# Two graph layers on one core: wk and wv loaded behind the first turn of x, q computed before k, and all places written anew

## The chip, the cores and the metric

The kernel runs on one core of one Trainium2 chip. The metric is the device time of one execution in microseconds (us), as the median of several runs. The core has a matmul engine (PE, with its weight loads PEld), a vector engine (DVE), a scalar engine (ACT), GpSimd (POOL) and SyncE (SP), which here only issues transfers (DMAs).

## The reference, cut to what is computed

```python
# x: (128, 128, 512) float32, adj: (128, 128) of zeros and ones
q, k, v = (x @ Wq + bq), (x @ Wk + bk), (x @ Wv + bv)        # 8 heads of 64
scores = einsum('bqhd,bkhd->bhqk', q, k) / sqrt(64) + (1 - adj) * -1e9
x = layernorm(x + einsum('bhqk,bkhd->bqhd', softmax(scores), v) @ Wo + bo)

h = x @ W                                                    # (512, 512)
s1, s2 = h @ a[:512], h @ a[512:]
e = leaky_relu(s1[:, :, None] + s2[:, None, :], 0.2) * adj
h_prime = softmax(e, axis=2) @ h
x = layernorm(x + elu(h_prime + beta * h))
```

The output has the shape of x. All is float32.

## The kernel before

The 128 batches (b) are worked on in 64 pairs (g, with b0 and b1). For a pair and each of the five weights (q, k, v, w for Wo, h for W) the product of the 512-wide x of two batches with the weight is a 2 x 2 block product made of seven block products instead of eight: `product(name, g, n)` with n from 1 to 7 (L293 for v, w and h, L299 for q and k). Products 1 and 2 need only plain blocks of the weight and of x; the others need sums of blocks. `weight_sum(name, n, engine)` (L215 to L221) makes the sums of a weight once, on DVE for q and k and on POOL for v, w and h; `block_sum` (L252, POOL) makes those of x (tx), oT and zT for each pair. The results leave PSUM by `take_part` (ACT for q, k, v and h at L347 and L341, DVE for w at L344), with a first copy into qT, kT, v, y or h, and by `add_block` (L357, DVE), which adds a second block to it. The PSUM pool has 8 buffers, so a product also waits until an earlier result has been taken out. Seven block products of q or k are 8 matmul passes each.

A pair goes through these stages: x is fetched twice, once in blocks of 32 rows (`load_blocks` L81, tile xblk, one buffer, four transfers) which `turn_x` (L232, DVE, one call for each batch) transposes into xT, and once as rows (`load_x` L91); then the q and k products, `scores` (L371), `mask` (L379) and `row_max` (L387) on DVE, `exps` (L393) and `normalise` (L407) on ACT; the attention weights go to memory and come back (`attn_write` L414 and `attn_read` L419, issued by SP), and are turned by DVE (`turn_attn` L436); `attend` (L446) follows, the w products, a layernorm, the second layer's row sums (`row_product` L497, `s2_write` L540, `s2_read` L548), its weights (`weights_write`, `weights_read`), `aggregate` (L634), the h products, elu (`elu_max` L649 on DVE, `elu_exp` L645 on ACT), a layernorm (`norm_f` L664) and `store` (L670, SP). The stages of several pairs overlap.

The order on every engine is written by hand. `at(place, fn, args)` puts a step on a list with a place, a number; the list is sorted by place and executed in that order with the scheduler switched off, so each engine and each queue executes its instructions in order of place. A pair's steps are in `rows(g)`, in which the places count from `g * STEP` (36.678). Pairs 62 and 63 have `last_rows`, where w and h of the last pair are computed as plain products. The dictionary `other` gives pairs 0, 1, 2, 3, 60 and 61 other places for the same rows. Steps that happen once (weight sums, loads of later weights) have places of their own.

At the start, outside this list, SP issues the first x in blocks and then wq, wk and wv (each 1 MB, `load_turned` L99); ACT issues two more quarters of x; POOL issues the small inputs (adj, the biases, a). `keep_busy(20, "early")` (L137) gives PE matmuls on an identity matrix, 40 passes in the profile, until data come. The function `load_later` fetches the rows of the first batches. wo and w1 follow by `load_weight` (L121). `wa_column` (L179, DVE), `wa_turn` and `wa_centre` make the product of W with the vectors a, once.

Of the kernel before, what the change touches and what calls it, by code (L numbers as in the profile page):

```python
# [18 lines left out]
STEP = 36.678  # L19
# [3 lines left out]
def gnn_two_layers(  # L23
# [91 lines left out]
    load_turned(wk_sb, wk)  # L115
    load_turned(wv_sb, wv)
# [22 lines left out]
    keep_busy(20, "early")  # L139
# [65 lines left out]
    sums = {}  # L205

# [475 lines left out]
    def at(place, fn, *args):  # L682
        pieces.append((place, len(pieces), fn, args))

    def rows(g):

        b0, b1 = g * G, g * G + 1
        return (
            (-44.716, fetch_blocks, g), (-36.858, turn_x, g, 0), (-32.016, turn_x, g, 1),
            (-29.266, block_sum, "x", g, 1), (-28.714, block_sum, "x", g, 2),  # L690
            (-26.46, block_sum, "x", g, 4), (-25.056, block_sum, "x", g, 3),
            (-21.919, product, "q", g, 1), (-21.658, take_part, "q", g, 1, 0, 0),
            (-19.5, product, "k", g, 1), (-17.956, product, "q", g, 2),
            (-16.658, take_part, "k", g, 1, 0, 0), (-15.381, product, "q", g, 6),
            (-15.182, add_block, "q", g, 2, 0, 0), (-14.288, product, "k", g, 2),
            (-12.099, take_part, "q", g, 6, 1, 0), (-11.378, product, "k", g, 6),
            (-10.677, product, "q", g, 7), (-10.463, product, "k", g, 7),
            (-9.776, add_block, "k", g, 2, 0, 0), (-9.113, take_part, "k", g, 6, 1, 0),
            (-6.848, product, "q", g, 5), (-6.525, product, "k", g, 5),
            (-6.518, take_part, "q", g, 5, 1, 1), (-6.421, take_part, "k", g, 5, 1, 1),  # L700
            (-5.969, add_block, "q", g, 7, 1, 1), (-5.586, fetch_x, b0), (-5.534, fetch_x, b1),
            (-4.88, product, "q", g, 3), (-4.75, add_block, "k", g, 7, 1, 1),
            (-3.315, product, "k", g, 3), (-2.944, product, "q", g, 4),
            (-2.923, take_part, "k", g, 3, 0, 1), (-2.725, take_part, "q", g, 3, 0, 1),
            (-1.262, product, "k", g, 4), (-0.719, add_block, "k", g, 4, 1, 0),
            (-0.692, add_block, "q", g, 4, 1, 0), (1.869, residual, b1), (2.023, scores, b0),
            (2.943, scores, b1), (3.203, product, "v", g, 1), (3.463, mask, b0, 0),
            (3.487, mask, b0, 1), (3.658, row_max, b0), (4.555, exps, b0, 0),
            (5.075, mask, b1, 0), (6.271, residual, b0), (6.383, product, "v", g, 2),
            (6.541, exps, b0, 1), (7.568, take_part, "v", g, 1, 0, 0), (7.611, exps, b0, 2),  # L710
            (8.122, product, "v", g, 7), (8.183, mask, b1, 1), (8.41, product, "v", g, 6),
            (8.797, exps, b0, 3), (8.894, add_block, "v", g, 2, 0, 0),
            (8.955, take_part, "v", g, 6, 1, 0), (9.854, row_inv, b0),
            (10.401, normalise, b0, 0), (10.555, normalise, b0, 1), (10.857, normalise, b0, 2),
            (11.052, row_max, b1), (11.513, normalise, b0, 3), (11.654, attn_write, b0),
            (11.776, product, "v", g, 5), (12.497, exps, b1, 0), (13.24, exps, b1, 1),
            (15.283, attn_read, b0), (16.447, exps, b1, 2), (17.972, exps, b1, 3),
            (18.187, row_inv, b1), (20.285, normalise, b1, 0), (20.649, normalise, b1, 1),
            (20.984, normalise, b1, 2), (22.744, normalise, b1, 3), (22.805, attn_write, b1),
            (24.259, turn_attn, b0, 0), (25.642, take_part, "v", g, 5, 1, 1),  # L720
            (25.922, attn_read, b1), (28.935, add_block, "v", g, 7, 1, 1),
            (30.213, product, "v", g, 3), (30.509, product, "v", g, 4),
            (31.14, take_part, "v", g, 3, 0, 1), (31.481, turn_attn, b0, 1),
            (31.923, add_block, "v", g, 4, 1, 0), (32.495, turn_attn, b1, 0),
            (32.689, turn_attn, b1, 1), (35.816, attend, b0), (36.86, attend, b1),
            (37.764, attend_evict, b0), (38.489, attend_evict, b1),
            (40.162, block_sum, "w", g, 1), (40.287, block_sum, "w", g, 3),
            (40.532, product, "w", g, 1), (41.714, product, "w", g, 2),
            (43.07, block_sum, "w", g, 2), (43.121, take_part, "w", g, 1, 0, 0),
            (43.685, block_sum, "w", g, 4), (44.107, add_block, "w", g, 2, 0, 0),  # L730
            (46.18, product, "w", g, 6), (47.336, take_part, "w", g, 6, 1, 0),
            (47.833, product, "w", g, 7), (48.561, product, "w", g, 5),
            (49.902, take_part, "w", g, 5, 1, 1), (50.317, add_block, "w", g, 7, 1, 1),
            (51.85, product, "w", g, 3), (52.678, take_part, "w", g, 3, 0, 1),
            (52.954, product, "w", g, 4), (53.025, bn_stats, y, b1, "c"),
            (54.273, add_block, "w", g, 4, 1, 0), (54.685, bn_stats, y, b0, "c"),
            (56.257, bn_aggr, b1, "c"), (57.446, bn_aggr, b0, "c"), (57.581, add_eps, g, "c"),
            (57.665, inv_std, g, "c"), (57.668, row_product, b1, 0),
            (57.799, row_product, b0, 0), (59.124, row_product, b1, 1),
            (59.504, row_product, b0, 1), (59.697, scale_s, g), (59.806, s2_turn, g),  # L740
            (61.509, s2_write, g), (63.81, norm_c, b0), (63.847, s2_read, g),
            (65.062, norm_c, b1), (69.697, edge, g, 0), (70.127, edge, g, 1), (70.179, leaky, g),
            (70.643, edge_max, g), (72.113, edge_exp, g), (73.622, edge_inv, g),
            (74.481, weights, g, 0), (75.191, weights, g, 1), (76.181, weights_write, g),
            (78.597, weights_read, g), (84.328, weights_turn, g), (85.331, aggregate, b0),
            (86.702, aggregate, b1), (87.456, aggregate_evict, b0),
            (88.848, aggregate_evict, b1), (89.224, block_sum, "h", g, 1),
            (90.935, product, "h", g, 1), (92.58, take_part, "h", g, 1, 0, 0),
            (92.618, block_sum, "h", g, 2), (93.008, product, "h", g, 2),
            (95.183, product, "h", g, 6), (95.377, block_sum, "h", g, 3),  # L750
            (95.522, take_part, "h", g, 6, 1, 0), (96.049, product, "h", g, 5),
            (96.355, product, "h", g, 7), (96.647, add_block, "h", g, 2, 0, 0),
            (98.71, block_sum, "h", g, 4), (99.498, take_part, "h", g, 5, 1, 1),
            (100.462, add_block, "h", g, 7, 1, 1), (101.867, product, "h", g, 4),
            (102.513, product, "h", g, 3), (102.514, take_part, "h", g, 3, 0, 1),
            (102.524, add_block, "h", g, 4, 1, 0), (103.384, elu_max, b0), (103.53, elu_exp, b0),
            (104.737, elu_max, b1), (107.392, elu_exp, b1), (118.64, elu_sum, b0),
            (120.181, bn_stats, u, b0, "f"), (121.875, elu_sum, b1), (122.064, bn_aggr, b0, "f"),
            (124.368, bn_stats, u, b1, "f"), (124.757, bn_aggr, b1, "f"),
            (125.543, add_eps, g, "f"), (129.855, inv_std, g, "f"), (131.762, shift, g),  # L760
            (132.875, norm_f, b1), (133, norm_f, b0), (133.412, store, b1), (133.946, store, b0),
        )

    def last_rows(g):

        b0, b1 = g * G, g * G + 1
        if g == NG - 2:
            return (
                (-44.716, fetch_blocks, g), (-36.858, turn_x, g, 0), (-32.016, turn_x, g, 1),
                (-29.266, block_sum, "x", g, 1), (-28.714, block_sum, "x", g, 2),  # L770
                (-26.46, block_sum, "x", g, 4), (-25.056, block_sum, "x", g, 3),
                (-20.581, product, "q", g, 7), (-19.688, product, "q", g, 1), (-18.819, fetch_x, b0),
                (-18.555, take_part, "q", g, 1, 0, 0), (-17.929, product, "k", g, 1),
                (-17.919, fetch_x, b1), (-17.036, product, "k", g, 7), (-16.143, product, "k", g, 2),
# [261 lines left out]

    for g in range(NG):
        lay(g)
    at(-0.85, load_later)
    at(7.15, make_mask)  # L1040
    at(7.47, weight_sum, "k", 3, nc.vector)
    at(8.19, weight_sum, "k", 1, nc.vector)
# [69 lines left out]
```

## Time and profile before

| | us |
|---|---|
| three runs | 2390.34, 2392.12, 2392.55 |
| median | 2392.12 |
| profiled execution, whole time | 2389.93 |
| its span (the profile's time axis) | 2388.1 |
| PE busy | 2359.0 (99%) |
| DVE, ACT, POOL busy | 79%, 66%, 36% |
| period of a middle pair | 36.50 |
| first product of x on PE | 13.12 |
| last matmul ends | 2379.43 |

The time axis of the profile begins with the program. In the lists of PE in order of time a line has the start, the time taken, engine, line of the code, output and inputs, how many instructions it holds, and in brackets the idle time ahead of it and what ended it. In a table of stretches each engine has its busy time and the number of instructions, then follow the granted clock of PE (1.00 is full speed), the busy share of the 16 DMA engines and GB/s. In a list of waits the numbers are us in total, times, longest.

### The profile page before, as it was taken

Reading aid. Unit: us, or ns where it says so; the run is one execution under the profiler, and the core shown is the slowest. Engines: PE = TensorE matmul, PEld = TensorE weight load, DVE = VectorE, ACT = ScalarE, POOL = GpSimd, SP = SyncE. Lnnn points to the kernel's source line nnn. Section 1 sums busy time; section 2 is a strip of 40 time slices with the busy share of each in tenths; the row PEclk is TensorE's granted clock in tenths of the full one; section 3 lists DMA queues with packets and bytes.
Section 4 is the critical chain, followed back from the end, with each engine's and each line's share of the span. In section 5 each row is a group of like instructions: output and inputs, shape, how many; then the busy total and the mean of one; then the engine's idle time right before and its main releaser. Section 6 shows DMA issues by size and latency. Waiting matters only on the chain.

```text
span 2388.1 us, 50634 instructions
## 1 busy us (share of the span) xinstructions
PE 2359.0 (99%) x17708; PEld 2179.7 (91%) x17708; DVE 1876.4 (79%) x4381; ACT 1583.2 (66%) x5760; POOL 867.2 (36%) x1047
## 2 busy tenths in 40 slices
PE   8999999999999999999999999999999999999998
PEld 7898999999999999999999999999999999999985
DVE  6787787877877877878778778778788787787877
ACT  4676766766666666667666676676676666766655
POOL 6242433433433334334334333343343343333421
PEclk9999999999999999999999999999999999999999
DMA  6333334344343343343433433433434334334332
GB/s 191 103 95 115 108 104 132 92 120 124 101 119 114 103 125 105 106 132 93 120 121 103 119 112 105 125 100 111 133 91 120 117 107 118 107 111 125 118 100 73
DMA packets 255905, 269.82 MB, mean 113 GB/s; under 512 B 57425, under 2 KB 204369, under 8 KB 255265
## 3 DMA queue, kind: packets, MB, share of 16 engines
q1 hardware_dynamic: 254704, 265.45, 37.0%
q8 instruction: 140, 2.29, 0.4%
q14 instruction: 117, 0.95, 0.1%
q0 software_dynamic: 400, 0.86, 0.1%
q10 hardware_dynamic: 544, 0.26, 0.0%
HBM read 157.62 MB, written 108.85 MB: 112 GB/s over the span
## 4 chain that ended last, share of the span: by engine, by line
PE 95%; DMA 2%; DVE 1%; ACT 1%; SPq 0%; issue 0%; DVEq 0%; ACTq 0%
PE pv L293 12%; PE pk L299 12%; PE pq L299 11%; PE pw L293 11%; PE ph L293 11%; PE eq L299 9%; PE psc L371 5%; PE po L446 5%; PE pz L634 5%; PE ew L293 4%; PE ev L293 4%; PE eh L293 4%; DMA scr<-sb 1%; ACT sb L407 1%; DMA ab<-scr 1%; DMA wk_sb<-in_L_gnn_Wk_dram 0%
## 5 line engine op out<-in xcount | busy, mean ns | idle before, releaser
L393 ACT ACTIVATE s<-s,nmax 128x128 f32<-128x128 f32 x1024 | 398.1, 395 | 150.1 <-DVE nmax L387 150.1
L427 POOL TENSOR_TENSOR x<-x,bo_b_in 128x512 f32<-128x512 f32 x128 | 163.8, 1280 | 892.6 <-DMA x<-in_x_dram 769.9
L407 ACT ACTIVATE sb<-s,rinv 128x128 f32<-128x128 f32 x1024 | 319.5, 395 | 2.9 <-DMA scr<-sb 2.6
L347 ACT ACTIVATE kT<-pk,bk_c 128x128 f32<-128x128 f32 x512 | 160.6, 367 | 194.1 <-PE pk L299 151.5
L341 ACT COPY h<-ph 128x256 f32<-128x256 f32 x252 | 94.6, 376 | 258.4 <-PE ph L293 257.1
L347 ACT ACTIVATE qT<-pq,bq_c 128x128 f32<-128x128 f32 x512 | 159.2, 364 | 89.7 <-PE pq L299 89.3
L393 ACT ACTIVATION_READ_ACCUMULATOR s<-s,nmax 128x1 f32 x1024 | 196.9, 192 | 0.0
L252 POOL TENSOR_TENSOR th<-zT,zT 128x256 f32<-128x256 f32 x63 | 46.3, 736 | 395.5 <-ACT zT L641 395.5
L379 DVE SCALAR_TENSOR_TENSOR s<-psc,amask 128x512 f32<-128x512 f32 x256 | 167.6, 676 | 27.6 <-PE psc L371 27.3
L344 DVE TENSOR_TENSOR w<-pw,x 128x256 f32<-128x256 f32 x252 | 103.2, 410 | 101.0 <-PE pw L293 100.9
L497 DVE SCALAR_TENSOR_TENSOR ya<-w,wa_row 128x512 f32<-128x512 f32 x256 | 177.6, 694 | 4.4
L436 DVE STREAM_TRANSPOSE attnT<-ab 128x512 f32<-128x512 f32 x256 | 172.6, 694 | 7.4 <-DMA ab<-scr 6.5
L458 ACT ACTIVATE oT<-po,bv_c 128x128 f32<-128x128 f32 x512 | 139.6, 382 | 27.7 <-PE po L446 27.7
L387 DVE TENSOR_REDUCE nmax<-s 128x8 f32<-128x1024 f32 x128 | 153.5, 1199 | 2.3
L232 DVE STREAM_TRANSPOSE xT<-xblk 128x512 f32<-128x512 f32 x128 | 143.1, 1120 | 5.2 <-DMA xblk<-in_x_dram 5.2
L299 PEld LDWEIGHTS pk<-xT,wk_sb 128*128 128x128 f32 x1024 | 136.0, 195 | 10.6 <-issue 4.2
L299 PE MATMUL pk<-xT,wk_sb 128*128 128x128 f32 x1024 | 136.9, 278 | 4.1 <-DMA wk_sb<-in_L_gnn_Wk_dram 4.1
L293 PE MATMUL pv<-wv_sb,xT 128*128 128x256 f32 x512 | 137.6, 391 | 0.0
L299 PE MATMUL pq<-xT,wq_sb 128*128 128x128 f32 x1024 | 134.8, 275 | 0.0
L299 PEld LDWEIGHTS pq<-xT,wq_sb 128*128 128x128 f32 x1024 | 129.4, 192 | 3.3
L371 PE MATMUL psc<-kT,qT 64*128 64x128 f32 x2048 | 131.8, 278 | 0.0
L371 PEld LDWEIGHTS psc<-kT,qT 64*128 64x128 f32 x2048 | 119.4, 188 | 11.5 <-issue 11.3
(674 smaller groups left out, 6297.0 us busy)
## 6 DMA issues: line engine op xcount, KB each, us to landing
scr<-sb SPq DMA_DIRECT2D x128, 512.0 KB
ab<-scr SPq DMA_DIRECT2D x512, 128.0 KB
x<-in_x_dram SPq DMA_DIRECT2D x128, 256.0 KB
out_dram<-u SPq DMA_DIRECT2D x128, 256.0 KB
xblk<-in_x_dram SPq DMA_DIRECT2D x254, 128.0 KB
pb<-s2d SPq DMA_DIRECT2D x62, 128.0 KB
attd<-att SPq DMA_DIRECT2D x62, 128.0 KB
ab<-attd SPq DMA_DIRECT2D x248, 32.0 KB
```

Source lines behind the costliest of these rows:

```text
L232: nc.vector.transpose(xT[g][:, :, t * N : (t + 1) * N].rearrange("p m (b r) -> p b m r", r=Q), xblk[g][:, t].rearrange("p b (c m) -> p b m ...
L293: nc.tensor.matmul(out, b[:, c, :], a[:, c, :], start=first and c == 0, stop=(c == 1), skip_group_check=True,)
L299: nc.tensor.matmul(out[:, m * N : (m + 1) * N], a[:, c, m * P : (m + 1) * P], b[:, c, :], start=first and m == 0 and c == 0, stop=(c == 1) ...
L347: nc.scalar.activation(dst[:, m, :], src[:, m * N : (m + 1) * N], AF.Identity, bias=BIAS[name][:, 2 * i + m : 2 * i + m + 1],)
L371: nc.tensor.matmul(psc[b][j][:, m, :], qT[g][feats, m, rows], kT[g][feats, m, rows], start=True, stop=True,)
L379: nc.vector.scalar_tensor_tensor(s_t[b][:, j * HP : (j + 1) * HP, :], psc[b][j], SCALE, amask.rearrange("p (o n) -> p o n", o=1).broadcast ...
L387: nc.vector.tensor_reduce(nmax[b], s_t[b], AX.X, ALU.max, negate=True)
L393: nc.scalar.activation(s_t[b][:, h, :], s_t[b][:, h, :], AF.Exp, bias=nmax[b][:, h : h + 1], accum_out=rsum[b][:, h : h + 1],)
L407: nc.scalar.mul(sb[b][:, :, h, :], s_t[b][:, h, :].rearrange("p (b c) -> p b c", c=Q), rinv[b][:, h : h + 1],)
L427: nc.gpsimd.tensor_tensor(xr[b], xr[b], later["bo"], ALU.add)
L436: nc.vector.transpose(attnT[b].rearrange("p h (a r) -> p a h r", r=Q)[:, rows], ab[b].rearrange("p a (h c) -> p a h c", c=Q)[:, rows],)
L497: nc.vector.scalar_tensor_tensor(z, y[b], 1.0, wa_row[j], ALU.mult, ALU.mult, accum_out=s12[g][:, i, j : j + 1])
```

## The change

Four things are changed, all in the function that the profile's lines belong to.

1. At the front only wq is loaded. wk and wv are loaded by a new step, which first writes one element of wk's tile in each partition on DVE, so that SP's transfer of wk waits for that instruction. Its place puts it between pair 0's two `turn_x`.
2. `keep_busy(20, "early")` becomes 15.
3. In pair 0 the q products come first: q1, q2, q7, then k1, k2, q6, k7, k6, q5, k5, q3, k3, k4, q4. On DVE the sums of wq come before those of wk. w1 is loaded before wo. The first of pair 1's `turn_x` stands ahead of the additions of q7 and k7 and of products k4 and q4; the first wa_column stands ahead of the additions of k4 and q4. The rows of b0 are fetched directly behind wv.
4. All places are other numbers: those of `rows(g)`, so of every middle pair, of `last_rows`, and of the six pairs in `other`. STEP is the same. The steps are the same, each with the same instructions.

In the middle pairs, for example, the order of the q and k products is q1, k1, q2, q6, k6, k2, q7, k7, q5, k5, q3, k3, q4, k4, where it was q1, k1, q2, q6, k2, k6, q7, k7, q5, k5, q3, k3, q4, k4. Near the end, the attn_read of batch 123 is ahead of an s2_write on SP, and on ACT q5's part is ahead of the elu_exp of batch 118, where each was behind it.

```diff
     load_turned(wq_sb, wq)
-    load_turned(wk_sb, wk)
-    load_turned(wv_sb, wv)
...
-    keep_busy(20, "early")
+    keep_busy(15, "early")
...
+    def load_k_and_v():
+
+
+        nc.vector.memset(wk_sb[:, 0, :1], 0.0)
+        load_turned(wk_sb, wk)
+        load_turned(wv_sb, wv)
...
     def rows(g):
-            (-44.716, fetch_blocks, g), (-36.858, turn_x, g, 0), (-32.016, turn_x, g, 1),
-            (-29.266, block_sum, "x", g, 1), (-28.714, block_sum, "x", g, 2),
...
+            (-44.347, fetch_blocks, g), (-35.5, turn_x, g, 0), (-35.24, turn_x, g, 1),
+            (-33.234, block_sum, "x", g, 1), (-29.664, block_sum, "x", g, 2),
...
     for g in range(NG):
         lay(g)
-    at(-0.85, load_later)
-    at(7.15, make_mask)
-    at(7.47, weight_sum, "k", 3, nc.vector)
...
-    at(10.35, weight_sum, "q", 3, nc.vector)
...
-    at(15.55, load_weight, wo_sb, wo)
...
-    at(18.25, load_weight, w1_sb, w1)
...
-    at(26.53, wa_column, 1, 0)
+    at(0.672, load_later)
+    at(5.774, load_k_and_v)
+    at(8.812, weight_sum, "q", 3, nc.vector)
...
+    at(13.252, weight_sum, "k", 3, nc.vector)
...
+    at(16.882, load_weight, w1_sb, w1)
...
+    at(19.582, load_weight, wo_sb, wo)
...
+    at(22.002, wa_column, 0, 1)
```

## The prediction

> **What bounds the kernel now.** I read the busy shares by slice, then PE's busy time by stretch, then what PE waited for, then PE in order of time.
>
> ```profile
> PE   8999999999999999999999999999999999999998
> ...
> DMA  6333334344343343343433433433434334334332
> ```
> ```profile
> core 0: us, PE busy (x) PEld busy (x) DVE busy (x) ACT busy (x) POOL busy (x), PEclk, DMA share, GB/s
> 0.00:13.12 13.12, 6.36 (x40) 6.19 (x41) 2.42 (x4) 1.28 (x1) 8.76 (x21) 0.99 0.84 271
> 13.12:60.00 46.88, 43.77 (x369) 40.90 (x369) 39.42 (x67) 24.23 (x93) 28.26 (x25) 0.97 0.59 168
> 60.00:240.00 180.00, 175.77 (x1329) 162.62 (x1330) 137.25 (x319) 117.31 (x438) 59.02 (x72) 0.99 0.35 104
> 240.00:2240.00 2000.00, 1999.99 (x15085) 1857.73 (x15084) 1584.51 (x3724) 1353.47 (x4933) 727.80 (x877) 1.00 0.38 113
> 2240.00:2379.43 139.43, 133.15 (x890) 112.30 (x889) 109.36 (x261) 84.78 (x293) 42.34 (x52) 0.99 0.29 95
> 2379.43:2388.10 8.67, 0.00 (x0) 0.00 (x0) 3.42 (x11) 2.16 (x3) 1.08 (x2) 0.64 0.16 60
> ```
>
> TensorE is the bound: in the 2000 us of the middle pairs it lacks 0.01 us, so nothing can be won there, only lost. The rest can be listed: 13.12 before the first product, 3.11 idle to 60, 4.23 to 240, 6.28 to the last matmul, 8.67 behind it.
>
> ```profile
> PE pk L299 <- DMA wk_sb<-in_L_gnn_Wk_dram: 4.1, 1, 4.1
> PE ph L293 <- ACT h L341: 3.4, 4, 2.2
> PE pk L299 <- ACT kT L347: 3.0, 2, 1.9
> ...
> PE pq L299 <- ACT qT L347: 2.5, 1, 2.5
> ```
> ```profile
> 2.70 6.36 PE L137 MATMUL early<-ident 128*128 128x128 f32 x40 [2.70 <-POOL ident masks.py:199]
> 13.12 3.57 PE L299 MATMUL pk<-xT,wk_sb 128*128 128x128 f32 x16 [4.07 <-DMA wk_sb<-in_L_gnn_Wk_dram]
> 17.46 1.13 PE L299 MATMUL pk<-tx,s_k 128*128 128x128 f32 x8 [0.76 <-issue]
> 18.43 1.95 PE L299 MATMUL pq<-xT,wq_sb 128*128 128x128 f32 x16
> ```
>
> The start is a wait for wk: the chain of waits has "DMA wk_sb" from 2.15 to 12.99. wq, issued first, is used only at 18.43. The first 16 passes take 3.57 where 16 warm ones take 1.79 on the chain (clock 0.50 in 13 to 16).
>
> **What the Trainium skill says.** (1) "TensorE: Matmul & The Clock Gate", section "What's actually happening": the clock is halved by default and after an idle window of about 3.4 us, and the window runs freely, so the gap that triggers it varies. The trace agrees and is sharper: gaps of 4.07, 2.47 and 2.16 us were followed by a clock of 0.50, 0.50 and 0.55, gaps of 1.89 and 1.07 by 1.00. (2) "DMA: Bandwidth & Descriptors", "Why a DMA increments its semaphore by 16 and not by 1": a transfer counts as landed only when all its engines are done, and these finish independently. The trace shows this: wk landed at 12.99, though at the mean rates (277 GB/s from 2 to 8, 368 from 8 to 13) the bytes ahead of its end had passed earlier. (3) Same page, "Queues, rings and completion order": an engine takes the descriptors of one queue in ring order. So moving wk's issue on SP back, behind nothing but x and wq, costs only as far as an engine runs dry; no row shows this.
>
> **The change, part by part.** The sum is made against the profiled execution, 2389.93; the median is 2392.12, so 2.2 is added at the end.
>
> *Early passes, 40 to 30.* They ran at 6 to 7 a microsecond to about 6 us and some 11 after, so 30 end near 6.9. Nothing waits for the ten: worth 0 while PE waits for data; their cover is the load of wq.
>
> *q in front of k.* wq is then the first weight. Its landing isn't shown; q1 had moved 1.40 MB by 8.0, against 1.31 for x's half and wq, so I take 8.5 (7.7 to 9.4). Products 1 and 2 of q (1.79) and 7 (0.89) run by 11.3: 2.68 us of work in what was idle. Both remaining gaps are about 1.7, which stayed warm before.
>
> *wk and wv behind a memset.* The memset (one element a partition, estimate 0.1) stands on DVE between the two turns of x, 1.08 us each, the first at 5.24. SP's issue of wk waits for it, so moves from 2.15 to about 6.4, with wv, the second batch of x, four xblk_1 and w1 queued behind it on SP. xblk_1 was issued at 7.35 and goes to about 7.9. At 6.4 the rings still hold half of wq, so I keep wk's landing at 13.0; bounds: 12.3 (two loads no longer interleave with wq) and 17 (the full 4.25).
>
> *From 13.0 on.* Before, 112 passes stood between wk and v1, with 1.78 of cold clock and 0.76 of issue; now 88. Nine products by 0.893 end at 21.0 (k1, k2, q6, k7, k6, q5, k5, q3, k3). Then comes a new wait. The order on DVE is now: turn of pair 1 (waits for xblk_1), add q7, add k7, and k4 needs their place in PSUM. xblk_1 used to be first-quarter landed at 19.90 and was turned at 24.48 without a wait; now it lies behind all of wv, estimate 21.6 (21 to 24). So k4 starts at 21.6 + 1.09 + 2 x 0.42 = 23.5: a gap of 2.5, cold with one chance in two (0.5 x 1.7 = 0.9). k4, q4 1.79, v1 0.86, q1 of pair 1 0.89: scores at 27.0 against 29.39, with one product of 0.89 more behind it: -3.2. wa_column now waits for w1 behind wv on the same DVE; w1 is due near 24.7, add k4 and add q4 stand behind it, and this just fits; not counted.
>
> *To 60.* 44.44 (0.45) and 51.06 (1.89) are stalls of the old order of pair 1, whose ACT order is new; I count the 1.89 as gone. **Start: -3.2 - 1.9 + 0.9 = -4.2**, between -6.5 and 0.
>
> *60 to 240.* Idle 4.23 and 1.7 of cold behind
>
> ```profile
> 217.47 0.48 PE L293 MATMUL ph<-s_h,th 128*128 128x256 f32 x1 [2.16 <-ACT h L341]
> ```
>
> 5.9 in all. The copy of h stood on ACT behind normalise, norm_f and a q/k part. In the new order of pairs 2 to 4 these are spread otherwise, but k6 and q5 follow close on their parts; I keep two thirds as lost: **-2.0**, between -5.9 and +3.
>
> *Middle pairs.* Every place is new, the instructions are the same. The tightest new distance on PE is k3 behind k5's part: 1.76 us of products between them against 0.2 + 0.63 of ACT. Scores, attend and aggregate have over 2 us. DVE is busy 79% and ACT 68% of a period of 36.5. **0**, between 0 and +17 (0.3 a pair); below nothing is excluded by 0.01 us idle.
>
> *End.* The largest stall:
>
> ```profile
> 2278.22 0.63 ACT L645 ACTIVATE h<-h 128x512 f32<-128x512 f32 x1 [3.51 <-DVE u L649]
> ```
> ```profile
> 2276.90 0.71 DVE L436 STREAM_TRANSPOSE attnT<-ab 128x512 f32<-128x512 f32 x1 [3.00 <-DMA ab<-scr]
> ```
>
> DVE waited 3.00 for an attn_read that SP issued at 2272.43 behind two stores (2.03) and an s2_write (1.03); elu_max stood behind it, elu_exp behind that, q5's part behind that on ACT, and PE waited 2.47 and ran cold (1.7). In the new order the read is ahead of the s2_write and q5's part ahead of elu_exp: -4.2. What is late next isn't known: the last five pairs have other new orders, with 3.8 of small stalls now. I take half: **-2.0**, between -5 and +4. The 8.67 behind the last matmul is the same chain of elu_sum, statistics, norm_f and store: 0.
>
> Sum -4.2 - 2.0 + 0 - 2.0 = -8.2: profiled run 2381.7, median 2383.9, say 2384.0.
>
> **The rivals.** *No gain (A):* the start is bound by bytes, not by their order: the DMA share is 0.97 to 1.12 from 2 to 31 us, and wk, wv, xblk_1, w1 and wo are the same bytes. Then xblk_1 lands at its bound of 24, k4 starts at 25.9, runs cold (1.7), and after 3.54 us of k4, q4, v1 and q1 the scores begin at 31.1: 0.9 late against 29.39 + 0.89. With the 1.89 gone the start gives -1.0; pairs 1 to 3 and the end find other stalls of the old size: 2389.93 - 1.0 + 2.2 = 2391.1. For it: the share. Against it: the 2.68 us of q work that no later byte delays.
>
> *Slower (B):* one new wait in the repeated order. A place on ACT or DVE that is late by 0.1 us in each middle pair costs 0.1 x 56 = 5.6 and leaves 2.6 of the gains; from 0.15 a pair (8.4) the kernel is slower, and at 0.25 it is 14.0 - 8.2 = +5.8: 2398. For it: PE has no slack to hide anything (1999.99 of 2000), and attention's round trip of write (2.6 to 4.6) and read (3.7) is measured against a new place of turn_attn. Against it: the old middle order shows no wait at all at the same busy shares, and I find no new distance shorter than its work.
>
> *Full gain (C):* xblk_1 in time, gaps warm, no new stalls outside: -6.5 - 5 - 4 = 2376.6.
>
> *The issue doesn't move (D):* were SP to issue wk early all the same, nothing would be lost, since q still starts first: 2384, the forecast.
>
> **How the numbers follow.** Forecast and C together 0.62 (C 0.12), A 0.25, B 0.13. 0.2%, 4.8 us, is about what a measurement of this kernel can tell from no change: faster is below 2387.3, slower above 2396.9. Forecast and C lie below, A between, B mostly above. The range leaves out half of C and most of B: 2376.5 to 2392.5.
>
> **What would show it.** First pass of q near 8.5, first of k near 13.0, both at clock 1.00; a wait of 2 to 3 us on DVE for xblk_1 and of k4 on DVE near 21 to 23.5; scores near 27; 2000.0 busy of 2000 in the middle; no stall on "ACT qT" near 2279. Wrong, if wk lands past 14, if the middle shows idle PE over 3 us, or if the last 140 us hold more than 6.3 of idle.

## The result, and the profile after

| | before | after |
|---|---|---|
| median, us | 2390.45 (6 runs, 2390.21 to 2392.55) | 2383.07 (6 runs, 2380.52 to 2384.31) |
| profiled execution, us | 2389.93 | 2381.98 |
| its span, us | 2388.1 | 2380.2 |
| last matmul ends | 2379.43 | 2372.0 |

The ratio is 0.9965 (95% interval 0.9953 to 0.9978): 7.4 us faster by the medians, 7.9 by the spans. The forecast was 2384.0, or 8.2 less than the kernel before.

PE's busy time by stretch, of the kernel after; the columns are those of the table shown of before:

```profile
core 0: us, PE busy (x) PEld busy (x) DVE busy (x) ACT busy (x) POOL busy (x), PEclk, DMA share, GB/s
0.00:8.50 8.50, 5.79 (x27) 5.79 (x28) 2.11 (x3) 0.32 (x1) 7.18 (x19) 1.00 0.73 202
8.50:60.00 51.50, 44.59 (x374) 41.29 (x373) 39.63 (x69) 25.42 (x94) 29.68 (x27) 0.97 0.63 188
60.00:240.00 180.00, 178.23 (x1350) 164.90 (x1349) 146.74 (x325) 119.13 (x450) 64.46 (x77) 1.00 0.36 106
240.00:2230.00 1990.00, 1990.00 (x15029) 1849.02 (x15028) 1654.71 (x3712) 1357.31 (x4915) 724.78 (x872) 1.00 0.37 113
2230.00:2372.00 142.00, 136.67 (x926) 115.89 (x924) 112.83 (x267) 88.38 (x301) 43.84 (x52) 1.00 0.34 102
```

The middle has no idle PE at all, as before. The lost time is idle time and the time that passes at half clock take too long, about 1.7 us behind each gap that ended cold. 13.12 and 10.12 are the times of the first product. By stretch it compares so:

| stretch | before | after | difference | forecast |
|---|---|---|---|---|
| to 60 us, early passes counted as lost | 13.12 + 3.11 + 1.8 = 18.0 | 10.12 + 5.79 + 1.7 = 17.6 | -0.4 | -4.2 |
| 60 to 240 | 4.23 + 1.7 = 5.9 | 1.77 | -4.2 | -2.0 |
| middle | 0.01 | 0.00 | 0 | 0 |
| end, to the last matmul | 6.28 + 1.7 = 8.0 | 5.33 | -2.7 | -2.0 |
| behind it | 8.67 | 8.2 | -0.5 | 0 |

The sum, -7.8, is nearly that of the forecast; its parts are not. The stretch to 240 gave twice what was forecast, the end somewhat more than forecast, and the start next to nothing. PE in the order of time, at the start of the kernel after:

```profile
2.71 6.29 PE L135 MATMUL early<-ident 128*128 128x128 f32 x30 [2.71 <-POOL ident masks.py:199]
10.12 2.02 PE L304 MATMUL pq<-xT,wq_sb 128*128 128x128 f32 x16 [1.12 <-DMA wq_sb<-in_L_gnn_Wq_dram]
14.39 2.05 PE L304 MATMUL pk<-xT,wk_sb 128*128 128x128 f32 x16 [1.35 <-DMA wk_sb<-in_L_gnn_Wk_dram]
...
24.11 1.13 PE L304 MATMUL eq<-tx,wk_sb 128*128 128x128 f32 x8 [0.71 <-DVE kT L362]
...
27.82 2.06 PE L376 MATMUL psc<-kT,qT 64*128 64x128 f32 x32
...
45.44 1.65 PE L298 MATMUL ev<-wv_sb,tx 128*128 128x256 f32 x4 [3.38 <-DVE v L362]
```

The first product starts 3.0 us sooner, PE stays at full clock after both first gaps, and the scores come at 27.82 instead of 29.39 with one product more done: up to there it goes much as forecast. Then PE waits 3.38 us for the addition of v7 and runs at half clock after it (0.57 from 45.4 to 49). What DVE did until then:

```profile
22.20 1.12 DVE L237 STREAM_TRANSPOSE xT<-xblk 128x512 f32<-128x512 f32 x1 [2.55 <-DMA xblk<-in_x_dram]
...
26.29 0.93 DVE L177 SCALAR_TENSOR_TENSOR wa_t<-w_sb,uf_in 128x512 f32<-128x512 f32 x1 [1.30 <-DMA w_sb<-in_L_gnn_W_dram]
...
38.59 1.66 DVE L177 SCALAR_TENSOR_TENSOR wa_t<-w_sb,uf_in 128x512 f32<-128x512 f32 x1
...
41.81 1.49 DVE L197 TENSOR_SCALAR wa_row<-wa_row,wa_mean 128x512 f32<-128x512 f32 x1
```

It waited 2.55 us for xblk_1 (the first blocks of pair 1), as forecast, and 1.30 us for w1, which landed at 26.19 where 24.7 was due. From there to the addition of v7 it hardly pauses, 18.64 us busy of 19.10, and PE is busy for 15.76:

```profile
26.30:45.40 19.10, 15.76 (x128) 14.38 (x126) 18.64 (x34) 11.54 (x50) 15.34 (x13) 1.00 0.45 118
```

In the same stretch of the kernel before DVE is busy for 15.84 us and PE for 18.65. The chain of waits that ends at the product at 45.44 runs over DVE from 26.3 on, but for 3.20 us of exps, and behind that over the landing of w1 (14.94 to 26.19). So w1 sets when DVE begins, and DVE's queue sets when PE goes on.

### The profile page after: what moved, and what is told of

Same layout as the page of the kernel before. It is cut to its first block, busy times and chain, and to the rows that moved or that the text cites. A ratio compares the mean times of both kernels' runs of the same rounds, so it can differ in the third digit from the quotient of the medians.

```text
span 2380.2 us, 50849 instructions
## 1 busy us (share of the span) xinstructions
PE 2355.3 (99%) x17698; PEld 2176.9 (91%) x17698; DVE 1959.5 (82%) x4382; ACT 1592.1 (67%) x5760; POOL 871.4 (37%) x1047
## 4 chain that ended last, share of the span: by engine, by line
PE 95%; DVE 2%; DMA 1%; ACT 1%; SPq 0%; issue 0%; ACTq 0%; DVEq 0%
PE pv L298 12%; PE pq L304 12%; PE pk L304 11%; PE pw L298 11%; PE ph L298 11%; PE eq L304 9%; PE psc L376 5%; PE po L451 5%; PE pz L639 5%; PE eh L298 5%; PE ew L298 4%; PE ev L298 4%; DMA w_sb<-in_L_gnn_W_dram 0%; ACT s L398 0%; DVE wa_t L177 0%; PE plh L333 0%
## 5 line engine op out<-in xcount | busy, mean ns | idle before, releaser
L412 ACT ACTIVATE sb<-s,rinv 128x128 f32<-128x128 f32 x1024 | 325.7, 392 | 5.5 <-DVE rinv L405 4.4
L502 DVE SCALAR_TENSOR_TENSOR ya<-w,wa_row 128x512 f32<-128x512 f32 x256 | 225.2, 880 | 4.3
L346 ACT COPY v<-pv 128x256 f32<-128x256 f32 x256 | 94.5, 369 | 87.1 <-PE pv L298 60.6
L257 POOL TENSOR_TENSOR tx<-xT 128x256 f32<-128x256 f32 x128 | 95.9, 750 | 132.5 <-PE psc L376 106.4
L654 DVE SCALAR_TENSOR_TENSOR u<-h,x 128x512 f32<-128x512 f32 x126 | 87.1, 692 | 61.5 <-ACT h L346 59.3
L304 PEld LDWEIGHTS pk<-xT,wk_sb 128*128 128x128 f32 x1024 | 129.0, 192 | 4.7 <-DMA wk_sb<-in_L_gnn_Wk_dram 1.5
```

The lines of the kernel that those rows point to most:

```text
L304: nc.tensor.matmul(out[:, m * N : (m + 1) * N], a[:, c, m * P : (m + 1) * P], b[:, c, :], start=first and m == 0 and c == 0, stop=(c == 1) ...
L346: nc.scalar.copy(dst, src)
L412: nc.scalar.mul(sb[b][:, :, h, :], s_t[b][:, h, :].rearrange("p (b c) -> p b c", c=Q), rinv[b][:, h : h + 1],)
L502: nc.vector.scalar_tensor_tensor(z, y[b], 1.0, wa_row[j], ALU.mult, ALU.mult, accum_out=s12[g][:, i, j : j + 1])
```

## The experiments

In two kinds: single places of the change put into the kernel before, and single places of the kernel after undone or moved. Each was timed in turn with the kernel before on the same chip; its median differs from chip to chip (2389.6 to 2391.6), so the ratios are compared. Single executions of one kernel differ by more than some of these edits are worth (the kernel before took 2384.03 to 2392.91 in 46 runs on one chip), so a trace shows one execution, and a gain is read from the medians.

**The loads in front again.**

```diff
     load_turned(wq_sb, wq)
+    load_turned(wk_sb, wk)
+    load_turned(wv_sb, wv)
...
-    at(5.774, load_k_and_v)
```

> The kernel after, with wk and wv issued directly behind wq at the front again; all places and the q-first order stay. Theory (ring order): each DMA engine takes wq's descriptors first anyway, so the first q product stays at 10.1 us within 0.7, wk lands about 13.0 instead of 14.3, and the time is 2381 to 2384. Rival (interleaving): three loads in flight at once delay wq, the first q product starts at 11.5 or later, and the start gives back 1.5 us or more: 2385 to 2387.

Measured: 2381.44, ratio 0.9964 (0.9951 to 0.9976). The time is that of the kernel after.

```profile
11.30 3.47 PE L306 MATMUL pq<-xT,wq_sb 128*128 128x128 f32 x16 [2.70 <-DMA wq_sb<-in_L_gnn_Wq_dram]
```

The first q product started at 11.30, behind a gap of 2.70 that ended cold, where it was 10.12. That the loads delay each other is not shown by this: in a later run with all three in front it started at 10.17, and in three later ones with the deferral at 9.29, 10.18 and 11.01. wk was there without a wait when q was done. The scores came at 29.80, 2.0 later than in the kernel after, and yet the time is the same: where the kernel after waits 3.38 us for DVE and goes cold, this one waits 1.46 and 1.54 us for it and stays at full clock. The part that gave the change its name is worth nothing that these intervals, some 3 us to either side, can tell.

**The old start, the new middle and end; and the new end alone.** Both take the rows of both kernels and choose by pair:

```diff
+    new = lambda g: g >= 4        # first kernel;  g >= NG - 4 in the second
...
+        rows, last_rows, other = (
+            (rows_a, last_rows_a, other_a) if new(g) else (rows_b, last_rows_b, other_b)
+        )
```

> The front and pairs 0 to 3 of the kernel before, all later pairs (middle and end) of the kernel after. By the account of lost PE time in the two traces, stretch by stretch, the start to 240 us is worth 4.6 us of the 7.9 and the end 3.1: so 2387.3 against 2390.5 of before. Rival: the end's gain is tied to the start's order, or the switch of order between pairs 3 and 4 costs a stall: 2390 or more.

> The kernel before, with the new places in pairs 60 to 63 alone. If the middle pairs' new order is worth nothing, as the 1990.00 of 1990 us busy says, this equals the run with the old start and the new middle, 2387.3 within 1. Rival: the new middle order carries part of the gain (the DVE order that reaches the end), then this stays near 2390.

Measured: 2392.28, ratio 1.0012 (1.0004 to 1.0020), and 2393.77, ratio 1.0017 (1.0010 to 1.0023). Both were expected at 2387.3 and are slower than the kernel before. PE in order of time in the first of them, around the pairs where the orders meet:

```profile
174.09 1.13 PE L293 MATMUL pv<-wv_sb,tx 128*128 128x256 f32 x4 [1.38 <-ACT v L341]
...
225.36 1.10 PE L293 MATMUL ph<-s_h,th 128*128 128x256 f32 x4 [1.76 <-ACT h L341]
```

There are eight such waits between 147 and 255 us, 6.2 us in all, seven of them for a step on ACT; in the second, waits of 0.3 to 1.4 us stand from 2194 us on. Two orders that each run without a wait in the middle do not fit one another. Steps of several pairs interleave on ACT and DVE there, which is the likely reason; no run shows it by itself. So these kernels can't price a stretch. One thing can be read from the first: its end has the waits of the kernel after (1.54, 0.55, 0.16, 0.81 and 0.50 us; in the kernel after 1.50, 0.55, 0.46, 0.81 and 0.50, with one of 0.18) although its start is the old one. The end's gain doesn't hang on the start.

**wk issued ahead of wq, in the kernel before.**

```diff
-    load_turned(wq_sb, wq)
     load_turned(wk_sb, wk)
+    load_turned(wq_sb, wq)
```

> The kernel before with one exchange: wk is issued ahead of wq at the front; nothing else. Theory (the weight that is used first must be issued first): the first k product starts near 10.1 instead of 13.1, 24 passes run before the second weight lands at 13 to 14.4, and 3 to 5 us of the start are won: 2386 to 2387.5. Rival (the start is bound by bytes and by DVE behind them): the wait moves to q, wv or the wa columns and the time stays at 2390 within 1.2.

Measured: 2386.24 against 2389.73, ratio 0.9984 (0.9978 to 0.9991): 3.5 us, by the exchange of two lines.

```profile
11.00 2.02 PE L299 MATMUL pk<-xT,wk_sb 128*128 128x128 f32 x16 [0.66 <-DMA wk_sb<-in_L_gnn_Wk_dram]
...
25.10 1.16 PE L299 MATMUL eq<-tx,wq_sb 128*128 128x128 f32 x8 [1.07 <-DVE kT L357]
27.06 2.06 PE L371 MATMUL psc<-kT,qT 64*128 64x128 f32 x32
```

The first k product starts at 11.00, where five executions with the old front have it at 13.12, 14.43, 14.79, 14.23 and 13.99; the scores come at 27.06. "The weight that is used first must be issued first" holds, and it holds for q as for k: with q in front the first product came at 9.29 to 11.30. The interval of the 3.5 us is 2.2 to 5.3, and the trace is of a slow execution (2388.74, where the median is 2386.24). It shows less: product work of 44.1 us by 60 us (44.2 and 42.3 in two later runs with this front, mean 43.6), where the kernel after has 44.1 and the old front has 42.8 in the mean of five. By this measure the start of the kernel after gained as much as this front. The two traces don't show where the rest of the 3.5 us comes from.

**The early attn_read, in the kernel before** (pair 61's place of `attn_read, b1`):

```diff
-            20.031, 20.621, 21.491, 22.301, 20.131, 11.939, 25.821, 15.221, 31.089, 34.634,
+            20.031, 20.621, 21.491, 22.301, 20.131, 11.939, 23.37, 15.221, 31.089, 34.634,
```

> The kernel before with one place changed: the attn_read of batch 123 is issued on SP ahead of the two stores and the s2_write that stood before it. Theory: DVE's wait of 3.00 us for it goes, with it the 2.47 us of PE on q5's part and the cold clock behind (1.7): the end gains 3 to 4 us, PE loses under 0.3 us at that product, 2386 against 2390. Rival: another wait of the same place (ACT's elu_exp, the stores issued later) takes over: gain under 1 us.

Measured: 2385.29 against 2389.57, ratio 0.9983 (0.9976 to 0.9989): 4.3 us (2.6 to 5.7 by the interval). SP's own queue, and PE at the product that waited 2.47 us:

```profile
2268.45 1.75 SPq L419 DMA_DIRECT2D ab<-scr  x4
2270.30 2.13 SPq L670 DMA_DIRECT2D out_dram<-u  x2
```
```profile
2277.62 1.05 PE L299 MATMUL pq<-xT,s_q 128*128 128x128 f32 x8
```

The reads are issued before the stores instead of 4 us later; the product has no idle time before it and runs at full clock (1.05 for 8 passes, 2.08 before). The other waits of the end are those of before. This is the forecast's chain, from SP over turn_attn, elu_max and elu_exp to q5's part, shown by taking away its first link.

**The early h copy, in the kernel before** (pair 3's place of `take_part, "h", g, 1, 0, 0`):

```diff
-            78.597, 84.328, 85.331, 86.702, 89.795, 89.245, 91.197, 91.239, 94.567, 91.977,
+            78.597, 84.328, 85.331, 86.702, 89.795, 89.245, 91.197, 91.239, 93.6, 91.977,
```

> The kernel before with one place changed: pair 3's copy of the first h block stands on ACT ahead of batch 11's normalise instead of behind six of its eight. Theory: PE's wait of 2.16 us near 217 falls below 0.6, so it stays warm: 3.2 to 3.8 us gained, 2386.5 against 2390. Rival: normalise moves back 0.35 us and attend waits for the attention round trip instead: gain under 1.5 us.

Measured: 2387.52, ratio 0.9989 (0.9981 to 0.9997): 2.1 us (0.7 to 4.5 by the interval), between the two.

```profile
216.33 1.10 PE L293 MATMUL ph<-s_h,th 128*128 128x256 f32 x4 [0.41 <-ACT h L341]
```

The wait falls from 2.16 to 0.41 and PE stays warm, which is the 3.4 us of the theory; 0.91 of it come back at 241.71, where a v product waits for its copy on ACT, which it did not before.

**All three.** The edits are the three above.

> The kernel before with three edits only: wk issued ahead of wq, the early attn_read of batch 123, the early h copy of pair 3. Theory: the gains of the change sit in these three places and add up: 3.5 + 3.5 + 3.5 = 10.5, so 2379.5, no slower than the kernel after (2382). Rival: they overlap (a later stage waits for the same round trip in any case): 2384 or more.

Measured: 2381.97 against 2389.57, ratio 0.9965 (0.9953 to 0.9978). This is the ratio of the whole change. The single gains (3.5 + 4.3 + 2.1 = 9.9) don't quite add up to the 7.6 measured, within what the intervals allow; if the two others keep their size, 1.2 is left for the front. Where the change writes some 360 lines, mostly of places, the order of two loads and two numbers do as much.

This trace has also the plainest view of what DVE's wa columns cost beside POOL. DVE, and POOL in the same stretch:

```profile
38.39 0.69 DVE L179 SCALAR_TENSOR_TENSOR wa_t<-w_sb,uf_in 128x512 f32<-128x512 f32 x1
...
39.13 1.64 DVE L179 SCALAR_TENSOR_TENSOR wa_t<-w_sb,uf_in 128x512 f32<-128x512 f32 x1
```
```profile
38.50 1.71 POOL L217 TENSOR_TENSOR w_sb<-w_sb 128x512 f32<-128x512 f32 x1 [2.91 <-DVE wa_t L179]
40.29 1.63 POOL L219 TENSOR_TENSOR s_h<-w_sb 128x512 f32<-128x512 f32 x1
```

The first column has begun when POOL's sum starts, and keeps its 0.69 us; the sum behind it takes 1.71 where the same line took 1.27 alone. The second column begins beside that sum, takes 1.64 and ends 0.56 us after it. The Trainium skill, "SBUF — State Buffer", section "SBUF: two separate sides", says why: DVE and GpSimd share one pair of ports under an exclusive lock for a whole instruction, which a DVE instruction with two SBUF inputs and a GpSimd instruction that reads SBUF both need. The trace agrees. In the kernel after, four columns and one wa_row fell beside POOL's sums: 1.10, 1.63, 1.66 and 1.75 instead of 0.69, and 1.49 for wa_row where an execution of it with POOL idle took 0.49: 0.41 + 0.94 + 0.97 + 1.06 + 1.00 = 4.4 us of DVE's 18.64. (wa_row has one large input, so the rule of two inputs doesn't cover it; that it took longer is what the trace shows.)

This is not what sets the two kernels apart: in the kernel before three columns (1.22, 1.63, 1.66) and both wa_rows (1.05, 1.09) met POOL's sums as well, 3.6 us by the same sum.

**wa steps later, in the kernel after.**

```diff
-    at(34.572, wa_centre, 0)
-    at(36.632, wa_column, 1, 2)
+    at(38.6, wa_column, 1, 2)
+    at(39.843, wa_centre, 0)
```

> The kernel after; wa_centre 0 and wa_column (1,2), 4.8 us of DVE between 40.2 and 45.0, are moved behind the row_inv of batch 1 and the addition of v7. Theory (the length of DVE's queue holds the start): PE's wait of 3.38 us on 'DVE v' and the cold clock behind it go, 5 us at that point, of which 2 come back later as shorter waits: 2379. Rival (the start is held by what lands): the time stays at 2382 within 1.

Measured: 2382.02, ratio 0.9967 (0.9954 to 0.9979), no gain. PE in order of time:

```profile
15.14 2.05 PE L304 MATMUL pk<-xT,wk_sb 128*128 128x128 f32 x16 [2.94 <-DMA wk_sb<-in_L_gnn_Wk_dram]
...
50.22 1.50 PE L304 MATMUL eq<-tx,wq_sb 128*128 128x128 f32 x8 [2.07 <-DVE qT L362]
```

The wait of 3.38 is gone, but at 44.85 PE waits 1.09 us for the next addition to v, and at 50.22 it waits 2.07 us for an addition to q, which again ended cold (clock 0.61 to 53). DVE had the same work to do; only its order was changed.

**POOL's sums later, in the kernel after; and everything.**

```diff
-    at(35.352, weight_sum, "w", 4, nc.gpsimd)
-    at(37.362, weight_sum, "h", 3, nc.gpsimd)
...
+    at(44.99, weight_sum, "w", 4, nc.gpsimd)
+    at(44.991, weight_sum, "h", 3, nc.gpsimd)
```

> The kernel after; five weight sums on POOL (w4 and the four of h, 6.5 us) are moved behind the residuals, out of the stretch in which DVE makes the wa columns. Theory (DVE and POOL hold each other up): the wa columns near 36 to 45, 1.1 to 1.66 us in the kernel after, fall to 0.7, so DVE comes to the addition of v7 about 3.4 us sooner and PE's wait of 3.38 us falls below 0.5. Rival (the columns are long for another reason): they stay above 1.0 and the wait stays near 3. In time: 2379 to 2381 under the theory if nothing else takes over, 2382 under the rival.

> The kernel after with the wa steps moved back, the five POOL sums moved back, and in the end stretch the first turn of x of pair 63 behind the addition of h7 of pair 59. Theory: PE's waits of the start past 30 us fall below 2 us in all and the 1.50 us near 2267 falls to 0.4: 2378 to 2380. Rival (the landing of weights sets the start, whatever DVE does): only the 1.1 of the end is won, 2381 to 2382.

> The kernel after with all three loads in front again, the five POOL sums late and pair 63's first turn late, the wa steps where they are. Theory (the deferral of wk and wv is worth nothing): equal to the kernel with all steps late within 1 us, 2378 to 2381. Rival (it is worth its 1.2 us of earlier first product): 1 to 2 us slower than that.

Measured: ratios 0.9975 (0.9965 to 0.9986), 0.9964 (0.9951 to 0.9978) and 0.9968 (0.9955 to 0.9980). None is faster than the kernel after, and the first is, if anything, slower. Its edit did not make the condition that it was to test: POOL went on with three residuals (from 34.85, for 4.62 us) in place of the sums, so the columns still took 1.27, 1.64, 1.63 and 1.66. What the start would gain without these collisions is therefore not shown by any run. The end's part of the second and third also missed: the wait of 1.50 us near 2267 stayed at 1.50. Between the turn of x that was moved and the addition of h7 stands an addition to q which waits for ACT's copy, and that decides. In the second, PE's waits past 30 us in the start were still 1.00, 0.76 and 1.60 us: the wait at v7 was gone, and others came. With the loads deferred or not (0.9964 and 0.9968; the second leaves the wa steps where they were) there is no difference that the intervals would show.

**Two more edits to the kernel before.**

```diff
-    at(35.369, wa_centre, 0)
-    at(37.119, wa_centre, 1)
+    at(39.6, wa_centre, 0)
+    at(39.601, wa_centre, 1)
...
-            -13.895, -13.002, -10.083, -12.109, -10.976, -11.216, -9.553, -9.333, -14.788,
+            -13.895, -13.002, -12.62, -12.109, -10.976, -11.216, -9.553, -9.333, -14.788,
```

> The kernel before with the three small edits and two more: both wa_centre steps (5.2 us of DVE) behind the additions of v7, k2 and q7 of pairs 0 and 1, and pair 2's copy of the first k block on ACT ahead of batch 3's normalise. Theory: PE's waits of 1.90 us near 49 and 1.07 near 75, which the kernel with three edits still had, go below 0.4 each: 2.3 us less than with three edits, so a ratio near 0.9956 to the kernel before against 0.9965 with three, and faster than the kernel after. Rival (DVE's backlog or the landing of data moves the wait elsewhere): 0.9963 or more.

Measured: 2382.31, ratio 0.9965 (0.9951 to 0.9978): nothing more than with three. Both waits went, and in this execution, the slowest of the five, others stood in their place:

```profile
27.07 1.16 PE L299 MATMUL eq<-tx,wq_sb 128*128 128x128 f32 x8 [2.71 <-DVE kT L357]
49.35 1.10 PE L293 MATMUL ev<-s_v,tx 128*128 128x256 f32 x4 [2.15 <-DVE wa_row L196]
```

No kernel of this study beats the kernel after by more than the measurement can tell; four stand beside it, at ratios of 0.9964 and 0.9965.

## Why the prediction was right, point by point

*What bounds the kernel, and the middle at 0:* right. Every place of the middle pairs was new, and PE lost nothing in 1990 us, though DVE's busy share of the whole span rose from 79% to 82% (row_product alone takes 880 ns in the mean, 694 before). Rival B did not come. The two mixed kernels show that its mechanism is real: waits of up to 1.8 us where orders don't fit.

*Early passes:* the outcome was right, the reading wrong. 30 passes ended at 9.0 and not at 6.9. The counts of 6 to 7 and 11 in a microsecond count a pass in every slice that it touches; from start to start a pass takes 0.21 us at first and 0.11 after the switch, and in the kernel after the switch came only at 8.4 us. wq was used at 10.12, so the passes were covered. No run changes them alone, so that they cost nothing is read from this order in time.

*q first, and the landings:* wq landed at about 10.0 (8.5 was taken, 9.4 the bound) and wk at 14.35 (13.0; bound 17). Both were late, and wk past the 14 that the prediction named as a sign of being wrong; both gaps stayed warm, and the first product came 3.0 us sooner. The run with wk ahead of wq prices the mechanism at 3.5 us (2.2 to 5.3).

*From 13.0 on, -3.2:* the recorded pair has 29.39 - 27.82 + 0.89 = 2.5. Over the executions with the old front the scores begin at 29.39, 32.88, 31.09, 30.48 and 30.34, mean 30.8; with the deferred front, q first, at 27.82, 28.26, 28.29 and 30.40, mean 28.7: 2.1 + 0.89 = 3.0. The size was about right; xblk_1 was turned at 22.20 (21.6 taken) and k4 started at 24.1 (23.5). The gap ahead of k4 was 0.71 and warm where 2.5 was taken, since the k products before it came later with wk. So the 0.9 for a cold clock was not needed there.

*To 60, the step that failed:* "I count the 1.89 as gone", and of wa_column "this just fits; not counted". The 1.89 was gone. But it was read by its last releaser alone, ACT. In the kernel before, ACT itself had waited 2.89 us for DVE's addition to k, and that stood behind the wa steps on DVE, which did not pause from 37.0 to 50.3. From the chain of waits to that product:

```profile
42.72 1.67 DVE wa_t L179 x2
...
50.02 0.34 DVE kT L357
50.36 0.02 issue
50.38 0.64 ACT kT L347 x2
51.02 0.04 issue
51.06 1.16 PE pk L299 x8
```

So a new order on ACT left DVE's queue as it was, and DVE was not named as the next to be late. The landing of w1, 1.5 us later than taken, and the wait for xblk_1 brought DVE to 26.29 with all the wa steps still to do. It cost 3.38 us and 1.7 of cold clock at v7, where the term had -1.9 + 0.9. So the start gave -0.4 in the recorded pair, and of the five traces with the old front the recorded one starts soonest. The product work that PE had done by 60 us (busy less early passes) gives 42.1 to 43.8, mean 42.8, with the old front, and 43.0 to 44.1, mean 43.5, with the deferred one: about 0.7 us, still far from 4.2. Rival A had the right outcome for the start, by another cause: not bytes alone, but DVE behind them. That DVE holds the start is read from the chain and from the two edits that only moved its waits (the loads in front, the wa steps later); no run gave DVE less work there.

*60 to 240, -2.0:* mis-sized, -4.2 in the traces. The wait at 217 went with its cold clock, and of the two thirds that were to be lost again only waits of 0.95 and 0.69 came. The single edit shows the cause (the h copy behind normalise on ACT), worth 2.1 (0.7 to 4.5 by its interval).

*End, -2.0:* the chain was right and so was its size of -4.2: 4.3 (2.6 to 5.7) in the run with the early read alone. Of that the new order of the last pairs gives back 1.5 by waits of its own, the 1.50 at 2266.92 above all:

```profile
2267.18 1.75 SPq L424 DMA_DIRECT2D ab<-scr  x4
2269.03 1.03 SPq L545 DMA_DIRECT2D s2d<-s2x  x2
```

SP's queue of the kernel after: the read is ahead, as the new places have it.

*The sum:* -8.2 forecast, -7.9 by the spans of the profiled executions, -7.8 by the table. A start taken too well by 3.8 was balanced by the stretch to 240, the end and the work behind the last matmul, taken too poorly by 2.2, 0.7 and 0.5. That the total was hit so closely is luck: 3.8 too much and 3.4 too little cancelled.

## What to carry to other kernels

Where one engine is busy to 99%, list its few waits with the clock behind each, and cure each by the step that stands in its releaser's queue: two places and the order of two loads were worth as much here as all places written anew. Follow the chain behind the last releaser before calling a wait cured. Here stalls taken out of a stretch in which another engine had almost no idle time came back some microseconds later; look at that engine's busy time in the stretch before counting a wait as won. The two orders here, each made as a whole, could not be spliced to see which half pays.

## What the hardware showed beyond this

The gap that ends in a halved clock has no fixed length. The prediction called the trace "sharper" than the skill's page, on gaps of 2.16 and more that went cold and 1.89 that did not. In these runs a gap of 2.07 ended at 0.61 and one of 2.24 at 0.54, while ones of 2.15 and 2.94 ended at 1.00. Even the same wait goes both ways. For one copy of k on ACT, PE waited 1.89 to 1.91 us in five executions with the old front and stayed at 1.00; with wk in front it waited 1.90 and ran at 0.57 for the next 3.5 us. The kernel before, and the run with wk ahead of wq:

```profile
51.06 1.16 PE L299 MATMUL pk<-tx,wk_sb 128*128 128x128 f32 x8 [1.89 <-ACT kT L347]
```
```profile
49.28 1.62 PE L299 MATMUL pk<-tx,wk_sb 128*128 128x128 f32 x8 [1.90 <-ACT kT L347]
```

So the border drawn in the prediction falls. That the length alone doesn't decide fits the free-running window that the prediction takes from the page; the page's figure of about 3.4 us of idleness doesn't fit, since gaps from 1.90 us on were enough here, and the measurement decides. The fall can also come late: in the kernel with three edits the eight passes behind the same gap of 1.90 still ran warm (1.16), and the next eight took 1.67.

The same front does not land at the same time. In five executions the first k product of the old front started between 13.12 and 14.79 us, and the scores between 29.39 and 32.88. This is more than some of the edits here are worth, so a start is not to be judged by one profile.

The early passes have two speeds that the recorded clock doesn't show. A pass followed the last by 0.21 us at first and by 0.11 us from some moment on, which was near 6.2 us in the kernel before and 8.4 in the kernel after, with a recorded clock of 1.00 throughout. The ratio is that of cold and warm passes elsewhere (3.57 and 1.79 us for 16). So 30 passes took 6.29 us in one kernel and 40 took 6.36 in the other. Why the moment differs is open.
